# Layer 1's inverse lengths from logarithm and exponential, with three smaller moves between engines

## The chip, the cores and the metric

The kernel runs on one NeuronCore of one Trainium2 chip. The metric is the device time of one execution in microseconds (us), the median over several runs. The kernel's text is in Bass with the Tile framework: the program names tiles and operations, and the framework puts in the semaphores. In some stages the framework also chooses the order of the instructions on an engine; in others the program's own order is kept.

Five engines appear below. PE is TensorE (matrix products; PEld are its weight loads), DVE is VectorE, ACT is ScalarE, POOL is GpSimd, and SP issues most of the DMAs. A float32 matrix product of the program appears in the trace as two MATMUL passes with two weight loads.

## The reference

Four residual layers on x of shape (4, 56, 56, 256) in float32, each over a group-normalised input:

```python
x = x + _L0_conv_ref(_gn(x), ...)   # 7x7 neighbourhood attention, 8 heads
x = x + _L1_conv_ref(_gn(x), ...)   # dense graph over an image's tokens
x = x + _L2_conv_ref(_gn(x), ...)   # neighbourhood attention, two dilations
x = x + _L3_conv_ref(_gn(x), ...)   # shifted 7x7 windows, 8 heads
```

Nearly the whole change lies in layer 1, which sees each image as 3136 tokens of 256 channels:

```python
xn = x / jnp.maximum(jnp.linalg.norm(x, axis=-1, keepdims=True), EPS)   # EPS = 1e-12
A = jnp.einsum('bnc,cc,bmc->bnm', xn, W_adj, xn)
A = jnp.exp(5.0 * (A - jnp.max(A, axis=-1, keepdims=True)))
A = A * (1.0 - jnp.eye(n, dtype=A.dtype))
A = A / jnp.maximum(jnp.sum(jnp.abs(A), axis=-1, keepdims=True), EPS)
rowsum = jnp.sum(A, axis=-1, keepdims=True)
xW = jnp.einsum('bnc,dc->bnd', x, W_aff)
Ax = jnp.einsum('bnm,bmc->bnc', A, x)
AxW = jnp.einsum('bnc,dc->bnd', Ax, W_aff)
diff = rowsum * (xW + b_aff) - AxW
mu = jnp.mean(diff, axis=-1, keepdims=True)
var = jnp.mean((diff - mu) ** 2, axis=-1, keepdims=True)
y = (diff - mu) * jax.lax.rsqrt(var + LN_EPS) * ln_gamma + ln_beta
y = jnp.where(y > 0, y, LEAK * y)
```

The first line divides each token by its length; the lines with `mu` and `var` are a LayerNorm of each token. In layer 0 a query's softmax sum runs over the 49 neighbours, with zero keys outside the image.

## The kernel before

The whole program is one launch. `direct_blocks` computes the four layers one after the other over all four images, with the residual stream in DRAM between them. A flag at the end would start a slower fallback on values out of range; it does not run here.

**Layer 0** works on 128 tiles: 32 groups of seven image rows (`r`), four column tiles each (`t`, with 16, 12, 12 and 16 columns, so 112 or 84 queries). For each tile `attend_pairs` issues the logits (L1080), the exponentials (L1088 and L1090), a multiplication with the mask on POOL (L1091) and, one tile later, the products with the values and with ones (L1113); the product with ones gives the softmax sum. The keys of a tile lie in two pieces. `both` (L1102) adds the two exponentials of a tile on POOL, twice per tile, so that the product with ones need run only once; a tile marked `alone` skips it, and TensorE then runs that product over both pieces. Three tiles are `alone`. The framework chooses the order of the instructions here.

**The tail of layer 0** overlaps the start of layer 1. From group `ALONE` (29 of 0 to 31) on, `stream` takes one entry of the list made by `first_tokens` into the `fill` of each tile. `first_tokens` prepares image 0 of layer 1 in six chunks of 512 tokens and a short one, chunk `NC4`, which holds the last 64 tokens twice. `normal` applies the group norm and squares on ACT (L942, L1397) and adds the two halves of 128 channels on DVE (L1398). `lengths` multiplies the squares with a column of ones (L1406), one product per 128 tokens, which gives the squared lengths as a column; DVE takes a maximum with 1e-24 (L1407), POOL raises it to the power -1/2 (L1408) and writes it on the diagonal of a tile `dg` (L1409). `unit_length` multiplies `dg` by ones (L1425), which brings the inverse lengths to all partitions as a row, and DVE multiplies the tokens by it (L1426). `values` is the product with W_aff (L1418).

**Layer 1** runs over units: a unit is one tile `j` of 128 tokens against up to four tiles from `first` to `last`, and since the matrix is symmetric only `first >= j` is computed. For each unit, TensorE makes logits (L1561), transposes the exponentials (L1669), and multiplies them by `xw` both ways: `by_row` (L1683) into the row's own sum, `by_column` (L1688) into `ps_v`, which DVE adds to `acc` (L1593). ACT takes the exponential (L1564) and copies the transposes (L1672). The main loop, for unit k, does: a small step, the transposes of k, the logits of k+1, a small step, the products of k. After a tile's last unit `finish` makes the LayerNorm: DVE sums, scales and takes the moments (L1726 to L1737), POOL makes the inverse deviation (L1739); two ticks later `normal` subtracts and scales on DVE (L1742), POOL applies gamma and beta (L1743, L1744), and `leaky` (L1747) and `add` (L1754, L1762) follow. A tick comes after each column product.

The chunks of the next image are prepared in between. At `j` of 1, 4, 8, 12, 16, 19 and 23 `replace` loads a chunk, puts its two `normal` steps behind four empty ones in the list `ticks`, and puts its other steps into `small`, due 12 column or row pairs later (`done + 12`): two empty ones, `lengths`, then `values`. `normal` here is DVE (L945), a Square on ACT (L1499) and an addition of halves on POOL (L1500). `lengths` is as in `first_tokens` (L1506 to L1508) for all chunks, but only chunks 3, 4 and 5 take the diagonal and a product with ones (L1516, L1536, due two later). Chunks 0, 1, 2 and `NC4` (`by_dma`) write the inverse lengths to DRAM and read them back on all partitions (L1512, L1513, due 16 later). DVE then multiplies (L1538). If a unit needs a chunk that is not ready, `begin` runs its remaining steps at once. The orders of PE and DVE are the program's in this layer; those of ACT and POOL are chosen by the framework.

PSUM in layer 1 holds one bank `m` (`ps_m`) for small products, two each of `s`, `o` and `v`, and one `t`.

Of the kernel before, what the change touches and what calls it, by code (L numbers as in the profile page):

```python
# [31 lines left out]
NIMG = 4  # L32
# [19 lines left out]
TINY = 1e-12  # L52
NEG = -1e30
# [777 lines left out]
def direct_blocks(ctx: ExitStack, tc: tile.TileContext, d: dict, watch):  # L831
# [8 lines left out]


# [20 lines left out]
    gn_eps = const.tile([P, 1], FP, name="gn_eps")  # L862
    nc.vector.memset(gn_eps, GN_EPS)
    group = const.tile([P, P], FP, name="group")
# [13 lines left out]
    def ps_m():  # L878
        return psum_tile("m", m_bufs)
# [278 lines left out]
    def layer0(early, big, pool, begin_layer1):  # L1158
# [85 lines left out]
        def pair(r, t):  # L1244
# [37 lines left out]
            def quad(hq):  # L1282
                def keys(j, u):
# [6 lines left out]
                 for a in range(2)]  # L1290
            return dict(quads=[quad(0), quad(1)], nk=nk, nq=nq, mask=m[0], emask=m[1], first=gather, done=finish,
                        alone=r == ALONE - 1 and t == 3 or r == ALONE and t == 2 or r == NIMG * NB0 - 1 and t == 3,
# [77 lines left out]

    def first_tokens(few, keep, brief):
# [19 lines left out]
        def normal(c):  # L1391
            m, n, x = part(c)
            sq = box["sq"] = brief.tile([P, CC, 512], FP, tag="sq", name="sq1")
            with tc.issue_after(newest[1].ins):
                for h in range(CC):
                    normalise_act(x[:, h], x[:, h], known(1, 0), h)
            nc.scalar.activation(sq[:, :, :n], x, AF.Square)  # L1397
            nc.vector.tensor_tensor(sq[:, 0, :n], sq[:, 0, :n], sq[:, 1, :n], ALU.add)  # L1398

        def lengths(c):  # L1400
            m, n, x = part(c)
            pm = ps_m()
            rn = few.tile([P, 4, 1], FP, tag="rn", name="rn")
            dg = box["dg"] = few.tile([P, 4, P], FP, tag="dg", name="dg", bufs=1)
            for i in range(m):
                nc.tensor.matmul(pm[:, i:i + 1], lhsT=box["sq"][:, 0, i * P:(i + 1) * P], rhs=ones[:, 0:1], start=True, stop=True)  # L1406
# [15 lines left out]
        def unit_length(c):  # L1422
            m, n, x = part(c)
            pm = ps_m()
            nc.tensor.matmul(pm[:, :n], lhsT=ones, rhs=box["dg"].rearrange("p m k -> p (m k)")[:, :n], start=True, stop=True)  # L1425
            nc.vector.tensor_tensor(x, x, pm[:, :n].rearrange("p (o k) -> p o k", o=1).to_broadcast([P, CC, n]), ALU.mult)  # L1426
# [25 lines left out]
    def layer1(early, big, pool, first, late, next_layer):  # L1452
# [7 lines left out]
        shares = dram.tile([NIMG, (NB + 1) * P], FP, name="shares")  # L1460
# [17 lines left out]
        def tokens(b, c, ps_a=ps_m):  # L1478
# [4 lines left out]
            by_dma = c in (0, 1, 2, NC4)  # L1483
# [18 lines left out]
            def lengths():  # L1502
                pm, sq = ps_a(), box["x0"]
                rn = few.tile([P, 4, 1], FP, tag="rn", name="rn")
                for i in range(m):
                    nc.tensor.matmul(pm[:, i:i + 1], lhsT=sq[:, 0, i * P:(i + 1) * P], rhs=ones[:, 0:1], start=True, stop=True)  # L1506
                nc.vector.tensor_scalar_max(rn[:, :m, 0], pm[:, :m], TINY * TINY)
                nc.gpsimd.tensor_tensor(rn[:, :m, 0], rn[:, :m, 0], mhalf[:, 0:1].to_broadcast([P, m]), ALU.pow)  # L1508
                box["share"] = few.tile([P, 4, P], FP, tag="dg", name="dg", bufs=1)
                if by_dma:  # L1510
                    row = shares[b:b + 1, 4 * c * P:4 * c * P + n]
                    nc.sync.dma_start(out=row.rearrange("o (m p) -> p (o m)", p=P), in_=rn[:, :m, 0])  # L1512
                    nc.sync.dma_start(out=box["share"].rearrange("p m k -> p (m k)")[:, :n], in_=row.to_broadcast([P, n]))  # L1513
                    small.append((done + 16, unit_length, (b, c)))
                else:
                    nc.gpsimd.tensor_tensor(  # L1516
                        box["share"][:, :m, :], ident.rearrange("p (o q) -> p o q", o=1).to_broadcast([P, m, P]),
                        rn[:, :m, :].to_broadcast([P, m, P]), ALU.mult)
                    small.append((done + 2, unit_length, (b, c)))
# [11 lines left out]
            def unit_length():  # L1531

                share = box["share"].rearrange("p m k -> p (m k)")[:, :n]
                if not by_dma:
                    pm = ps_a()
                    nc.tensor.matmul(pm[:, :n], lhsT=ones, rhs=share, start=True, stop=True)  # L1536
                    share = pm[:, :n]
                nc.vector.tensor_tensor(xnT[:, :, 4 * c * P:4 * c * P + n], box["x"][:, :, :n],  # L1538
                                        share.rearrange("p (o k) -> p o k", o=1).to_broadcast([P, CC, n]), ALU.mult)
# [5 lines left out]
            return [load], [lambda h=h: normal(h) for h in range(CC)], [no_step] * 2 + [lengths] + steps  # L1545
# [168 lines left out]
        def finish(b, j):  # L1714
# [19 lines left out]
            mv = late.tile([P, 3], FP, tag="mv", name="mv1", bufs=7)  # L1734
# [85 lines left out]
        def replace(b, c):  # L1820
            if b < NIMG:
# [4 lines left out]
                ticks.extend([no_step] * 4 + normals[b, c])  # L1826
# [693 lines left out]
```

## Time and profile before

| quantity | value |
| --- | --- |
| time, median of 3 runs | 3722.86 us (3720.98 to 3726.05) |
| the profiled execution's own time | 3720.84 us |
| its span, first to last instruction | 3719.0 us |
| mean granted TensorE clock | 0.996 |
| ACT table loads in the trace | 1, of 1283 ns |
| layer 0 up to where `first_tokens` starts | 0 to about 615 us |
| layer 0's tail with `first_tokens` | about 615 to 708 us |
| layer 1 | about 708 to 2560 us |
| layers 2 and 3 | about 2560 to 3719 us |

In a group row of the profile, the numbers after the shapes are the count, the busy time in us and the mean duration of one in ns, then the idle time of the engine just before them and what ended it. In rows in order of time the first two columns are start and length in us; a bracket at the end gives the idle time before and its releaser. A busy TensorE overlaps its own passes, so what an instruction really occupies is read from start to next start.

### The profile page before, as it was taken

Reading aid. Unit: us, or ns where it says so; the run is one execution under the profiler, and the core shown is the slowest. Engines: PE = TensorE matmul, PEld = TensorE weight load, DVE = VectorE, ACT = ScalarE, POOL = GpSimd, SP = SyncE. Lnnn points to the kernel's source line nnn. Section 1 sums busy time; section 2 is a strip of 40 time slices with the busy share of each in tenths; the row PEclk is TensorE's granted clock in tenths of the full one; section 3 lists DMA queues with packets and bytes.
Section 4 is the critical chain, followed back from the end, with each engine's and each line's share of the span. In section 5 each row is a group of like instructions: output and inputs, shape, how many; then the busy total and the mean of one; then the engine's idle time right before and its main releaser. Section 6 shows DMA issues by size and latency. Waiting matters only on the chain.

```text
span 3719.0 us, 112489 instructions
## 1 busy us (share of the span) xinstructions
PE 3645.2 (98%) x48938; PEld 2480.5 (67%) x48938; DVE 2197.2 (59%) x4176; ACT 1479.4 (40%) x3137; POOL 1802.9 (48%) x1952
## 2 busy tenths in 40 slices
PE   8999999999999999999999999999999999999998
PEld 4666666677776777767777777776666666555554
DVE  5787777544445444554444643445777777677776
ACT  5666665422222222222222222223666666444443
POOL 4777777421235222352222521124877778455555
PEclk9999999999999999999999999999999999999999
DMA  6554444300011000100000000002455444544443
GB/s 223 167 162 138 142 127 139 112 7 24 23 29 33 18 19 19 30 28 23 19 19 23 28 15 11 11 20 78 121 139 145 135 135 127 157 135 133 132 133 100
DMA packets 278695, 304.95 MB, mean 82 GB/s; under 512 B 33670, under 2 KB 269578, under 8 KB 277838
## 3 DMA queue, kind: packets, MB, share of 16 engines
q1 hardware_dynamic: 276336, 297.43, 26.6%
q8 instruction: 386, 6.32, 0.7%
q0 software_dynamic: 1568, 0.16, 0.1%
q14 instruction: 117, 0.96, 0.1%
q10 hardware_dynamic: 288, 0.08, 0.0%
HBM read 205.04 MB, written 92.55 MB: 80 GB/s over the span
## 4 chain that ended last, share of the span: by engine, by line
PE 90%; DVE 4%; POOL 1%; DMA 1%; issue 1%; ACT 1%; SPq 0%; DVEq 0%; ACTq 0%; POOLq 0%
PE ps_m L952 19%; PE ps_o L1683 14%; PE ps_s L1561 14%; PE ps_v L1688 13%; PE ps_m L981 7%; PE ps_o L1113 6%; PE ps_s L1080 6%; PE ps_t L1669 3%; PE ps_o L1040 2%; PE ps_s L1024 1%; PE ps_m L1526 1%; DMA vp<-vd 1%; POOL b L1102 1%; PE ps_m L1418 1%; PE ps_m L1754 1%
## 5 line engine op out<-in xcount | busy, mean ns | idle before, releaser
L1593 DVE TENSOR_TENSOR acc<-acc,ps_v 128x257 f32<-128x257 f32 x1088 | 457.5, 422 | 774.8 <-PE ps_v L1688 751.8
L1688 PE MATMUL ps_v<-xw,e 128*128 128x257 f32 x2208 | 611.1, 381 | 3.5 <-DVE xnT L1538 2.2
L1683 PE MATMUL ps_o<-xw,at 128*128 128x257 f32 x2208 | 609.0, 379 | 0.0
L1561 PE MATMUL ps_s<-xnT,xd 128*128 128x512 f32 (+3 forms) x1344 | 571.4, 548 | 3.9 <-DVE xnT L1538 3.9
L1672 ACT COPY at<-ps_t 128x512 f32<-128x512 f32 (+3 forms) x332 | 170.4, 513 | 953.6 <-PE ps_t L1669 953.4
L1688 PEld LDWEIGHTS ps_v<-xw,e 128*128 128x128 f32 x2208 | 413.4, 189 | 145.0 <-issue 83.2
L1102 POOL TENSOR_TENSOR b<-e 124x448 f32<-124x448 f32 (+5 forms) x498 | 484.7, 994 | 7.2 <-PE ps_o L1113 0.3
L1683 PEld LDWEIGHTS ps_o<-xw,at 128*128 128x128 f32 x2208 | 419.1, 190 | 60.1
L952 PE MATMUL ps_m<-xn,w_wqkv 128*32 128x392 f32 x4096 | 374.3, 494 | 2.3 <-PE ps_s L1080 1.1
L1554 POOL TENSOR_SCALAR xd<-xnT,vec 128x128 f32<-128x128 f32 x192 | 116.1, 614 | 475.6 <-PE ps_s L1561 475.4
L1564 ACT ACTIVATE e<-ps_s 128x512 f32<-128x512 f32 x336 | 185.3, 552 | 354.4 <-PE ps_s L1561 351.1
L1561 PEld LDWEIGHTS ps_s<-xnT,xd 128*128 128x128 f32 x1344 | 225.4, 191 | 141.4 <-issue 126.2
L1091 POOL TENSOR_TENSOR e<-e,m0t 126x672 f32<-126x672 f32 (+3 forms) x128 | 238.7, 1865 | 158.6 <-ACT e L1090 126.2
L1091 POOL TENSOR_TENSOR e<-e,bias 119x784 f32<-119x784 f32 (+5 forms) x128 | 241.7, 1888 | 151.6 <-ACT e L1090 150.8
L1113 PEld LDWEIGHTS ps_o<-e,vp 124*32 124x32 f32 (+3 forms) x8192 | 198.0, 110 | 104.4 <-issue 85.3
L1002 ACT ACTIVATE no<-rs 128x168 f32<-128x168 f32 (+2 forms) x256 | 93.9, 367 | 385.8 <-DVE rs L2008 185.9
L952 PEld LDWEIGHTS ps_m<-xn,w_wqkv 128*32 128x32 f32 x4096 | 124.3, 109 | 176.5 <-issue 128.7
L2008 DVE RECIPROCAL rs<-ps_o 128x196 f32<-128x196 f32 (+2 forms) x128 | 175.7, 1373 | 103.6 <-PE ps_o L1113 83.4
L1113 PE MATMUL ps_o<-e,vp 124*32 124x112 f32 (+3 forms) x8192 | 227.6, 248 | 4.2 <-DMA vp<-vd 3.9
L1088 ACT ACTIVATE e<-e 126x672 f32<-126x672 f32 (+5 forms) x256 | 219.6, 858 | 17.4 <-DVE e L1087 5.0
L1090 ACT ACTIVATE e<-ps_s 126x672 f32<-126x672 f32 (+5 forms) x256 | 206.1, 805 | 8.6 <-PE ps_s L1080 6.4
L981 PE MATMUL ps_m<-w_wqkv,xn 128*32 128x256 f32 x3136 | 197.6, 381 | 3.8 <-DVE xr L2044 2.0
(235 smaller groups left out, 5973.6 us busy)
## 6 DMA issues: line engine op xcount, KB each, us to landing
x<-xr SPq DMA_DIRECT2D x64, 392.0 KB
x<-in_x SPq DMA_DIRECT2D x53, 448.0 KB
x<-x SPq DMA_DIRECT2D x60, 392.0 KB
xr<-x SPq DMA_DIRECT2D x60, 392.0 KB
vd<-v SPq DMA_DIRECT2D x72, 256.0 KB
xr<-in_x SPq DMA_DIRECT2D x32, 392.0 KB
xr<-x SPq DMA_DIRECT2D x28, 448.0 KB
x<-xr SPq DMA_DIRECT2D x28, 448.0 KB
```

What stands on the lines that cost most here:

```text
L952: nc.tensor.matmul(pm[j * HD:(j + 1) * HD, :n], lhsT=w[:, h, col + j * HD:col + (j + 1) * HD], rhs=rhs(h), start=(h == 0), stop=(h == CC - 1))
L981: nc.tensor.matmul(pm[i:i + HD, j * C:(j + 1) * C], lhsT=xn[:, h, first + i:first + i + HD], rhs=w[:, h, :], start=(h == 0), stop=(h == CC ...
L1080: nc.tensor.matmul(s[j // 2][:nk, j % 2, (2 * i + u) * nq:(2 * i + u + 1) * nq], lhsT=k(j, u), rhs=q(j), start=True, stop=True)
L1088: newest.append(nc.scalar.activation(ev, ev, AF.Exp))
L1090: nc.scalar.activation(ev, sv, AF.Exp)
L1091: nc.gpsimd.tensor_tensor(parts(ev), parts(ev), w["emask"], ALU.mult)
L1102: nc.gpsimd.tensor_tensor(w["b"][a][:nk, :, :2 * nq].rearrange("p h (i c) -> p h i c", i=2), ev[:, :, :, 0, :], ev[:, :, :, 1, :], ALU.add)
L1113: nc.tensor.matmul(w["o"](k, i)[j * HD:(j + 1) * HD], lhsT=ones[:nk, :HD] if k else v(j, u), rhs=w["b"][j // 2][:nk, j % 2, i * nq:(i + 1) ...
L1561: nc.tensor.matmul(s[:, :n], lhsT=xd[j][:, h, :], rhs=xnT[:, h, first * P:last * P], start=(h == 0), stop=(h == CC - 1))
L1593: nc.vector.tensor_tensor(acc[:, i, :], acc[:, i, :], pv[:, :C + 1], ALU.add)
L1683: nc.tensor.matmul(out[j][:, :C + 1], lhsT=e[:, col(i)] if i == j else at[:, col(i)], rhs=xw[:, i, :], start=(i == j), stop=(i == NB - 1))
L1688: nc.tensor.matmul(pv[:, :C + 1], lhsT=e[:, col(i)], rhs=xw[:, j, :], start=True, stop=True)
```

## The change

It has four parts and one load.

- **Lengths.** In both token paths the squares are multiplied by a full 128x128 tile of ones, so that the squared lengths come out on all partitions as a row at once. `inverse_lengths` takes Ln, with the argument scaled by 2^16, and then Exp of -1/2 times that plus 8 ln 2, on ACT. `shorten` takes the minimum with 1e12 and multiplies the tokens, in one DVE instruction. The maximum, the power, the diagonal, the second product and the way over DRAM go.
- **Halves.** In `first_tokens` the addition of the two halves on DVE goes; TensorE accumulates both halves in its product. In layer 1's `tokens` the addition on POOL stays.
- **Layer 0's last sums.** `alone` holds for the last 13 tiles, from group 28's last tile on, instead of for three.
- **LayerNorm.** `normal` in `finish` becomes one ACT instruction with a scale and a bias per token; POOL makes the bias, minus mean times inverse deviation.
- **Due times.** `unit_length` is due four pairs after `lengths` for all chunks, with an empty step behind `lengths`. The last chunk's `normal` comes after two empty ticks instead of four, and its other steps are due 7 pairs later instead of 12, without the two empty ones ahead of `lengths` (these also go for the short chunk).
- **Table load.** An explicit load of the ACT table set `natural_log_exp_and_others` is the first instruction of ACT.

```diff
+    tables = [s.name for s in act_sets.SETS].index("natural_log_exp_and_others")
+    nc.scalar.add_instruction(mybir.InstLoadActFuncSet(name=nc.get_next_instruction_name(), act_func_set_id=tables,
+                                                       ins=[], outs=[]))
...
-    gn_eps = const.tile([P, 1], FP, name="gn_eps")
+    offsets = const.tile([P, 2], FP, name="offsets")
+    gn_eps, half_ln = offsets[:, 0:1], offsets[:, 1:2]
     nc.vector.memset(gn_eps, GN_EPS)
+    nc.vector.memset(half_ln, LN_SCALE / 2 * float(np.log(2.0)))
...
-                        alone=r == ALONE - 1 and t == 3 or r == ALONE and t == 2 or r == NIMG * NB0 - 1 and t == 3,
+                        alone=NTC * r + t >= NTC * ALONE - 1,
...
+    def inverse_lengths(share, pm):
+        nc.scalar.activation(share, pm, AF.Ln, scale=float(2 ** LN_SCALE))
+        nc.scalar.activation(share, share, AF.Exp, scale=-0.5, bias=half_ln)
+
+    def shorten(dst, x, share):
+        n = share.shape[1]
+        nc.vector.scalar_tensor_tensor(dst, share.rearrange("p (o k) -> p o k", o=1).to_broadcast([P, CC, n]), 1 / TINY, x,
+                                       ALU.min, ALU.mult)
...
@@ first_tokens @@
             nc.scalar.activation(sq[:, :, :n], x, AF.Square)
-            nc.vector.tensor_tensor(sq[:, 0, :n], sq[:, 0, :n], sq[:, 1, :n], ALU.add)
...
-            for i in range(m):
-                nc.tensor.matmul(pm[:, i:i + 1], lhsT=box["sq"][:, 0, i * P:(i + 1) * P], rhs=ones[:, 0:1], start=True, stop=True)
-            nc.vector.tensor_scalar_max(rn[:, :m, 0], pm[:, :m], TINY * TINY)
-            nc.gpsimd.tensor_tensor(rn[:, :m, 0], rn[:, :m, 0], mhalf[:, 0:1].to_broadcast([P, m]), ALU.pow)
-            nc.gpsimd.tensor_tensor(dg[:, :m, :], ident.rearrange("p (o q) -> p o q", o=1).to_broadcast([P, m, P]),
-                                    rn[:, :m, :].to_broadcast([P, m, P]), ALU.mult)
+            for h in range(CC):
+                nc.tensor.matmul(pm[:, :n], lhsT=ones, rhs=box["sq"][:, h, :n], start=(h == 0), stop=(h == CC - 1))
+            box["share"] = few.tile([P, 4 * P], FP, tag="share", name="share", bufs=1)
+            inverse_lengths(box["share"][:, :n], pm[:, :n])
...
@@ tokens @@
+                nc.tensor.matmul(pm[:, :n], lhsT=ones, rhs=sq[:, 0, :n], start=True, stop=True)
+                box["share"] = few.tile([P, 4 * P], FP, tag="share", name="share", bufs=1)
+                inverse_lengths(box["share"][:, :n], pm[:, :n])
+                small.append((done + 4, unit_length, (b, c)))
...
+                shorten(xnT[:, :, 4 * c * P:4 * c * P + n], box["x"][:, :, :n], box["share"][:, :n])
...
-            return [load], [lambda h=h: normal(h) for h in range(CC)], [no_step] * 2 + [lengths] + steps
+            return [load], [lambda h=h: normal(h) for h in range(CC)], [no_step] * (2 if c < NC4 - 1 else 0) + [lengths, no_step] + steps
...
@@ finish @@
+            nc.gpsimd.tensor_scalar(mv[:n, 3:4], mv[:n, 0:1], rstd[:n], -1.0, ALU.mult, ALU.mult)
...
-                nc.vector.tensor_scalar(y, y, mv[:n, 0:1], rstd[:n], ALU.subtract, ALU.mult)
+                nc.scalar.activation(y, y, AF.Identity, bias=mv[:n, 3:4], scale=rstd[:n])
...
@@ replace @@
-                ticks.extend([no_step] * 4 + normals[b, c])
-                small[:0] = [(done + 12, step, (b, c)) for step in steps]
+                soon = c == NC4 - 1
+                ticks.extend([no_step] * (2 if soon else 4) + normals[b, c])
+                small[:0] = [(done + (7 if soon else 12), step, (b, c)) for step in steps]
```

More of the change, by code (lines that the diff above doesn't have):

```diff
@@ L20 @@
 import concourse.tile as tile
-from concourse import mybir
+from concourse import act_sets, mybir
 from concourse._compat import with_exitstack
@@ L52 @@
 TINY = 1e-12
+LN_SCALE = 16
 NEG = -1e30
@@ L1402, in lengths @@
             pm = ps_m()
-            rn = few.tile([P, 4, 1], FP, tag="rn", name="rn")
-            dg = box["dg"] = few.tile([P, 4, P], FP, tag="dg", name="dg", bufs=1)
-            for i in range(m):
-                nc.tensor.matmul(pm[:, i:i + 1], lhsT=box["sq"][:, 0, i * P:(i + 1) * P], rhs=ones[:, 0:1], start=True, stop=True)
-            nc.vector.tensor_scalar_max(rn[:, :m, 0], pm[:, :m], TINY * TINY)
-            nc.gpsimd.tensor_tensor(rn[:, :m, 0], rn[:, :m, 0], mhalf[:, 0:1].to_broadcast([P, m]), ALU.pow)
-            nc.gpsimd.tensor_tensor(dg[:, :m, :], ident.rearrange("p (o q) -> p o q", o=1).to_broadcast([P, m, P]),
-                                    rn[:, :m, :].to_broadcast([P, m, P]), ALU.mult)
+            for h in range(CC):
+                nc.tensor.matmul(pm[:, :n], lhsT=ones, rhs=box["sq"][:, h, :n], start=(h == 0), stop=(h == CC - 1))
+            box["share"] = few.tile([P, 4 * P], FP, tag="share", name="share", bufs=1)
+            inverse_lengths(box["share"][:, :n], pm[:, :n])
         def values(c, i0):
@@ L1423, in unit_length @@
             m, n, x = part(c)
-            pm = ps_m()
-            nc.tensor.matmul(pm[:, :n], lhsT=ones, rhs=box["dg"].rearrange("p m k -> p (m k)")[:, :n], start=True, stop=True)
-            nc.vector.tensor_tensor(x, x, pm[:, :n].rearrange("p (o k) -> p o k", o=1).to_broadcast([P, CC, n]), ALU.mult)
+            shorten(x, x, box["share"][:, :n])
             if c == NC4:
@@ L1459, in layer1 @@
         racc = big.tile([P, C + 1], FP, name="racc")
-        shares = dram.tile([NIMG, (NB + 1) * P], FP, name="shares")
         idx = big.tile([98, WN], I32, name="idx")
@@ L1482, in tokens @@
             n = m * P
-            by_dma = c in (0, 1, 2, NC4)
             box = {}
@@ L1503, in lengths @@
                 pm, sq = ps_a(), box["x0"]
[L1504 to L1519, printed above, removed]
+                nc.tensor.matmul(pm[:, :n], lhsT=ones, rhs=sq[:, 0, :n], start=True, stop=True)
+                box["share"] = few.tile([P, 4 * P], FP, tag="share", name="share", bufs=1)
+                inverse_lengths(box["share"][:, :n], pm[:, :n])
+                small.append((done + 4, unit_length, (b, c)))
             def values(i0):
@@ L1531, in unit_length @@
             def unit_length():
[L1533 to L1539, printed above, removed]
+                shorten(xnT[:, :, 4 * c * P:4 * c * P + n], box["x"][:, :, :n], box["share"][:, :n])
                 if c == NC4:
@@ L1733, in finish @@
             st = pool.tile([P, 6], FP, tag="st", name="st1")
-            mv = late.tile([P, 3], FP, tag="mv", name="mv1", bufs=7)
+            mv = late.tile([P, 4], FP, tag="mv", name="mv1", bufs=7)
             nc.vector.bn_stats(out=st[:n], in_=y)
```

## The prediction

> **What bounds the kernel now.** I read the page's first part, then the busy time by stage, then TensorE's waits inside the two stages that the change touches, then the instructions in order of time. First the page, its engines and its chain:
>
> ```profile
> PE 3645.2 (98%) x48938; PEld 2480.5 (67%) x48938; DVE 2197.2 (59%) x4176; ACT 1479.4 (40%) x3137; POOL 1802.9 (48%) x1952
> PE 90%; DVE 4%; POOL 1%; DMA 1%; issue 1%; ACT 1%; SPq 0%; DVEq 0%; ACTq 0%; POOLq 0%
> ```
>
> TensorE is busy for all but 74 us and makes 90% of the chain. Two things can move the time: TensorE work added or removed, and those 74 us with what they do to its clock. By stage (core 0: length, then busy time and instructions of PE, PEld, DVE, ACT, POOL, then granted clock, DMA share, GB/s):
>
> ```profile
> 0.00:615.00 615.00, 590.40 (x13476) 366.92 (x13480) 453.72 (x671) 378.93 (x891) 450.83 (x380) 1.00 0.50 156
> 615.00:708.00 93.00, 85.66 (x1410) 61.59 (x1402) 62.95 (x94) 46.00 (x83) 61.88 (x53) 0.93 0.33 102
> 708.00:2560.00 1852.00, 1837.98 (x8270) 1361.51 (x8271) 859.80 (x2225) 419.63 (x790) 537.94 (x796) 1.00 0.09 24
> ```
>
> The second row is layer 0's tail, where `first_tokens` runs; the third is layer 1. The tail has 7.3 us of idle TensorE (93.00 less 85.66) and a clock of 0.93, worth another 6.5 us (93 x 0.07). Layer 1 has 14.0 us idle, 12.4 of it in three like stretches, one at each image's end (4.23 in 1100 to 1230, 4.23 in 1570 to 1700, 3.95 in 2045 to 2170), with ACT busy 23% of the stage. TensorE's waits in the tail (total, times, longest) and two 5 us slices of the tail:
>
> ```profile
> PE ps_m L1406 <- DVE sq L1398: 3.5, 4, 1.2
> PE ps_m L1418 <- DVE xnT L1426: 1.3, 2, 1.0
> ...
> 635.00:640.00 5.00, 3.78 (x74) 3.26 (x78) 3.21 (x6) 2.80 (x4) 5.00 (x5) 0.91 0.52 154
> 640.00:645.00 5.00, 5.00 (x33) 4.08 (x30) 2.36 (x3) 2.72 (x6) 5.00 (x6) 0.50 0.29 99
> ```
>
> The largest wait is for the very addition of halves that the change takes from DVE. After the gaps before 640 the clock falls to 0.50, with POOL full.
>
> **The change, part by part.** Times are of the profiled execution: span 3719.0, its own time 3720.84, 2.0 below the median 3722.86.
>
> *Lengths in layer 1.* One matrix product of the program is two passes in the trace. The first image boundary shows both prices:
>
> ```profile
> 1146.54 1.02 PE L1536 MATMUL ps_v<-dg,ones 128*128 128x512 f32 x2
> 1147.39 0.49 PE L1669 MATMUL ps_t<-ident,e 128*128 128x128 f32 x3
> ...
> 1213.30 0.95 PE L1506 MATMUL ps_m<-ones,x 128*128 128x1 f32 x8
> 1214.11 0.64 PE L1669 MATMUL ps_t<-ident,e 128*128 128x128 f32 x4
> ...
> 1220.37 1.98 PE L1561 MATMUL ps_s<-xnT,xd 128*128 128x512 f32 x4 [1.31 <-DVE xnT L1538]
> ```
>
> From start to next start, four one-column products take 0.81 us, one 512-wide product 0.85. For images 1 to 3, chunks 3 to 5 go from 0.81 + 0.85 to 0.85: nine times -0.81, -7.3. Chunks 0, 1, 2, which had no wide product, go from 0.81 to 0.85: nine times +0.04, +0.4. In image 0 six chunks go from 1.66 to two wide products, 1.70: +0.2. The short chunks come out even. TensorE in layer 1: **-6.7**.
>
> *What hangs on it.* DVE's maximum (L1507, 0.16), POOL's power and diagonal (L1508, L1516, 1.02 and 1.04) and 24 DMA issues (L1512, L1513, 0.36 and 0.33 each on SP) go. They cost nothing today: the DMA share is 0.09 and the result was due 16 products later. ACT gains Ln and Exp, by the 128x512 Exp of L1564 (0.60 each): 1.2 us a chunk, 28 chunks, 34 us. Ln waits for the wide product. Behind it on ACT stand the copy of the transposes (L1672) and Exp of the logits (L1564), for which TensorE's row products and the next transposes wait. The cover: after its transposes TensorE has 1.72 us of logits and one column product (0.43) before it needs the copy. Where the next unit is one tile wide its logits take 0.45, and about 0.5 us is exposed; I charge +1.0 in all (0 to 34). `unit_length` on DVE now waits for ACT instead of TensorE; behind it stand the additions L1593, which free `ps_v` for L1688. Four products of distance (a row and a column product together 0.87 us) cover the 1.2 us. Its multiply (L1538, 1.21) becomes a three-operand one from SBUF; three-operand L1732 at 486 ns against two-operand L1742 at 426 for 256 elements suggests up to 14% more, 0.17 us x 21, hidden but at the boundaries.
>
> *Boundary stalls.* The last chunk's normalisation comes two ticks and its other steps five products sooner. Today they are forced one after the other between 1213 and 1220, ending in the 1.31 us wait above; with the work due earlier I take that off three times, -3.9 (0 to -3.9). The x tile is there: its load waits only for a buffer. Of the remaining 8.5 us, which wait for DVE (L1762, L1538, L1593), I take 2.6 off, a third, because DVE loses 0.43 us per tile (next part). Together **-6.5**, ends -12.4 and 0.
>
> *LayerNorm on ACT.* 100 multiplies leave DVE (L1742, 426 ns, 42 us) and enter ACT. ACT's L942 takes 703 ns at 392 and 753 at 448 elements with the same two vector operands, so 0.58 at 256: 58 us; ACT goes from 23% to 28% with the lengths. POOL gets 100 small products, 0.23 each by L926. All lies under TensorE's 98%. Only at the end of layer 1, where the trace's chain runs through POOL's L1739, L1743 and L1744 (2566 to 2573), is there less cover: 0.23 more on POOL and 0.15 on ACT, **+0.3**.
>
> *Layer 0's tail.* 13 tiles instead of 3 skip `both`. Ten tiles save 20 POOL additions (L1102, 0.9 to 1.15 us, 20 us of the 62 there), and TensorE sums both halves itself:
>
> ```profile
> 649.18 0.57 PE L1113 MATMUL ps_o<-b,ones 124*32 124x112 f32 x16
> 649.68 1.12 PE L1080 MATMUL ps_s<-q,kI 32*126 32x84 f32 x32
> ...
> 693.73 0.95 PE L1113 MATMUL ps_o<-e,ones 95*32 95x112 f32 x32
> 694.61 3.72 PE L1418 MATMUL ps_m<-w_waff,xnT 128*128 128x256 f32 x16
> ```
>
> 0.88 against 0.50 at 112 columns, +0.38; the same reading at 84 columns is 0.69 against 0.40, +0.29. Five tiles of each: **+3.4**.
>
> *The tail's stalls.* DVE's addition of halves ended 0.4, 1.1, 1.25 and 0.8 us after the Square that feeds it; without it the 3.5 us of waits fall by 2.7. POOL's 20 us of relief should take another 1.0 of the 7.3 us. I take **-3.7** (ends -7.3, 0). What is late next is the arrival of data: the chain there has 6.8 us of `vp` and 5.8 us of `xnT` transfers, which stay. If half the gaps go, I take half of the clock's loss with them, **-3.2**; ends -6.5 and +3.4 (one more half-clock stretch like that before 646).
> The Trainium skill, "TensorE: Matmul & The Clock Gate", section "HAM oscillation — how this bites in real kernels", puts the re-throttling at TensorE gaps above about 3.4 us. The longest wait here is 1.2 us and the clock fell all the same, so I keep the row; by the rule closing such gaps would return no clock, and the sum below would be -11.7.
>
> *The start.* The table load (1283 ns, now after ACT's two DMA issues) is put ahead of them, so `vec` lands 1.28 later, 5.4 instead of 4.1, and DVE's first statistics wait behind `qbias` until 5.55 instead of 4.89, less 0.24 of idle after it: **+0.5** (0 to 1.3).
>
> Sum: -6.7 + 1.0 - 6.5 + 0.3 + 3.4 - 3.7 - 3.2 + 0.5 = -14.9. 3720.8 becomes 3705.9; by the median 3722.9 it is **3708 us**.
>
> **The rivals.** *Only the arithmetic counts (3720).* Stalls move and do not shrink, since layer 0 is ordered by the framework anew and DVE still has its 4 us chains at the boundaries: -6.7 + 3.4 + 0.5 = -2.8. For it: waits of 0.2 to 1.3 us with seven different releasers. Against it: the largest is removed work.
> *ACT becomes late (3733 to 3747).* If the Ln/Exp pair stands uncovered in front of L1672, each of 28 chunks costs 1.2 us. With no boundary gain the rest is -6.7 + 0.3 + 3.4 - 3.7 - 3.2 + 0.5 = -9.4: slower than before from 8 uncovered chunks, beyond the measurement from 14 (+7.4); all 28 give +24, 3747; sixteen give +10, 3733. For it: strict order on ACT, one `m` bank, short units at the image ends. Against it: ACT idles 330 us before L1564 and 564 us before L1672.
> *The one table does not hold (up to 3780).* If Ln and Exp each load a table, 56 loads of 1283 ns are 72 us of ACT in the same place: 3708 + 72 = 3780 if exposed, 3708 if hidden. The trace has one load in all and cannot show it.
> The skill's "ScalarE: Activation LUTs", section "Table sets: the hidden batching unit", says that one set holds both functions and needs one load; no run here shows that yet.
>
> **How the numbers follow.** 0.2% is 7.4 us, about what a measurement of this kernel can tell from no change: faster is below 3715.4, slower above 3730.3. Forecast 0.64, arithmetic alone 0.18, ACT late 0.15, tables 0.03. Faster 0.64, same 0.19, slower 0.17. With every end at its best (-6.7 - 12.4 + 0.3 + 3.4 - 7.3 - 6.5 = -29.2) it is 3694; the forecast's own range is 3697 to 3715. Reaching over the arithmetic to the foot of the ACT case gives 3695 to 3730.
>
> **What would show it.** Right: no L1742 on DVE; one table load; about 150 one-column passes less in layer 1; layer 1's idle TensorE under 9 us, the 1.3 us wait for `xnT` gone; the tail's idle near 4 us at a clock near 0.96. Wrong: TensorE waiting for L1672's or L1564's successors behind Ln; further table loads; a tail with a lower clock; a layer 0 that is longer before 615.

## The result and the profile after

The changed kernel takes 3725.35 us (median of 19 runs, 3720.54 to 3731.55) against 3717.98 us for the kernel before (19 runs, 3714.01 to 3726.05): a ratio of 1.0018, 95% interval 1.0012 to 1.0024. It is slower, by about 7 us, where 3708 us and a gain were forecast. The profiled execution took 3724.74 us with a span of 3722.9.

The page's engines and its chain, after:

```profile
PE 3635.9 (98%) x48936; PEld 2464.1 (66%) x48936; DVE 2154.7 (58%) x4042; ACT 1562.6 (42%) x3293; POOL 1771.6 (48%) x1988
PE 90%; DVE 4%; ACT 1%; POOL 1%; DMA 1%; issue 1%; SPq 0%; DVEq 0%; ACTq 0%; POOLq 0%
```

TensorE works 9.3 us less than before, and the span is 3.9 us longer: what was saved came back as idle time. The two stages, in the same columns as in the prediction:

```profile
615.00:708.00 93.00, 84.58 (x1546) 59.42 (x1538) 62.92 (x84) 55.31 (x103) 29.84 (x23) 1.00 0.38 120
708.00:2560.00 1852.00, 1825.42 (x8104) 1344.83 (x8103) 817.15 (x2096) 489.39 (x920) 534.67 (x855) 1.00 0.07 22
```

In the tail the granted clock is 1.00 where it was 0.93, and POOL has 29.84 us of work where it had 61.88. In layer 1 TensorE idles 26.6 us (1852.00 less 1825.42) where it idled 14.0. Fixed slices shift against the work when something ahead gets shorter, so the stages are also told by the same instructions in both traces. Layer 1 runs from its first short unit's logits to its last row product:

| kernel | layer 1 begins | layer 1 lasts | layers 2 and 3 | span |
| --- | --- | --- | --- | --- |
| before | 708.7 | 1855.4 | 1154.9 | 3719.0 |
| after | 701.4 | 1865.4 | 1156.1 | 3722.9 |

The tail gained 7.3 us, layer 1 lost 10.0, and the layers after it 1.2. TensorE's waits in layer 1 (total, times, longest) tell where:

```profile
PE ps_m L1745 <- DVE xr L1753: 7.1, 6, 1.9
PE ps_m L1512 <- POOL x L1508: 6.0, 2, 3.0
PE ps_v L1678 <- DVE acc L1583: 3.8, 3, 1.5
PE ps_s L1551 <- DVE xnT L1385: 3.6, 3, 1.2
PE ps_v L1512 <- POOL x L1508: 3.0, 1, 3.0
```

New is the wait of the product of ones (L1512, the old L1506) for POOL's addition of halves: 3.0 us at each of the three image ends. The transposes of y wait 7.1 us for DVE's additions into `xr` where they waited 3.8 (L1745 and L1753 are the old L1754 and L1762). The wait for `xnT`, forecast to go, went from 3.9 to 3.6. The first image end in order of time shows the new one:

```profile
1192.70 1.00 DVE L951 TENSOR_SCALAR xn<-x,gst 128x512 f32<-128x512 f32 x2
1193.73 1.06 ACT L1507 ACTIVATE x<-xn 128x1024 f32<-128x1024 f32 x1 [3.37 <-DVE xn L951]
1194.87 1.26 POOL L1508 TENSOR_TENSOR x<-x 128x512 f32<-128x512 f32 x1 [7.54 <-ACT x L1507]
1196.18 1.13 PE L1512 MATMUL ps_m<-x,ones 128*128 128x512 f32 x2 [2.98 <-POOL x L1508]
```

The normalisation, the Square and the addition take 3.4 us one after the other (1192.70 to 1196.13). ACT and POOL were idle before theirs, and each starts within 0.1 us of what feeds it: the chain itself is the wait. TensorE stands from 1193.20. A slice just behind it, in the window view's columns:

```profile
1197.50:1200.90 3.40, 3.40 (x7) 1.50 (x6) 0.00 (x0) 1.65 (x3) 0.00 (x0) 0.50 0.59 154
```

For 3.4 us the granted clock is 0.50, which costs another 1.7 us. Layer 1 of the kernel before has no such slice; this one has two at the first image end. Between the first and the last instruction of layer 1 TensorE idles 13.5 us before and 27.5 after, which is 14.0 more, and is busy 1841.96 and 1837.88, which is 4.1 less with the half-clock time in it: together the 10.0 us. The waits account for the idle time: 9.0 (POOL) + 3.3 (`xr`) + 2.6 (`acc`) + 1.2 (copies into `acc`, not among the rows above) - 2.5 (`xnT`, for which the column products also waited 2.2 before) = 13.6.

### The profile page after: what moved, and what is told of

Same layout as the page of the kernel before. It is cut to its first block, busy times and chain, and to the rows that moved or that the text cites. A ratio compares the mean times of both kernels' runs of the same rounds, so it can differ in the third digit from the quotient of the medians.

```text
span 3722.9 us, 112433 instructions
## 1 busy us (share of the span) xinstructions
PE 3635.9 (98%) x48936; PEld 2464.1 (66%) x48936; DVE 2154.7 (58%) x4042; ACT 1562.6 (42%) x3293; POOL 1771.6 (48%) x1988
## 4 chain that ended last, share of the span: by engine, by line
PE 90%; DVE 4%; ACT 1%; POOL 1%; DMA 1%; issue 1%; SPq 0%; DVEq 0%; ACTq 0%; POOLq 0%
PE ps_m L958 19%; PE ps_s L1551 14%; PE ps_o L1673 14%; PE ps_v L1678 13%; PE ps_m L987 7%; PE ps_o L1119 6%; PE ps_s L1086 6%; PE ps_t L1659 3%; PE ps_o L1046 2%; PE ps_s L1030 1%; PE ps_m L1522 1%; PE ps_o L1637 1%; PE ps_s L1593 1%; PE ps_m L1745 1%; DMA vp<-vd 1%
## 5 line engine op out<-in xcount | busy, mean ns | idle before, releaser
L1108 POOL TENSOR_TENSOR b<-e 124x448 f32<-124x448 f32 (+4 forms) x478 | 463.9, 992 | 6.6
```

What stands on the lines that cost most here:

```text
L1108: nc.gpsimd.tensor_tensor(w["b"][a][:nk, :, :2 * nq].rearrange("p h (i c) -> p h i c", i=2), ev[:, :, :, 0, :], ev[:, :, :, 1, :], ALU.add)
```

## The experiments

Ratios are to the kernel before, timed on the same chip in the same batch, with 95% intervals. Medians of two kernels that are set beside each other can be of two batches; the kernel before had medians of 3716.9 to 3718.3 us in them. "Kernel 6" is the kernel of experiment 6. Line numbers move by a few between kernels.

**1. The old timing of the last chunk**, all else as changed.

```diff
-                soon = c == NC4 - 1
-                ticks.extend([no_step] * (2 if soon else 4) + normals[b, c])
-                small[:0] = [(done + (7 if soon else 12), step, (b, c)) for step in steps]
+                ticks.extend([no_step] * 4 + normals[b, c])
+                small[:0] = [(done + 12, step, (b, c)) for step in steps]
...
-            return [load], [lambda h=h: normal(h) for h in range(CC)], [no_step] * (2 if c < NC4 - 1 else 0) + [lengths, no_step] + steps
+            return [load], [lambda h=h: normal(h) for h in range(CC)], [no_step] * 2 + [lengths, no_step] + steps
```

> The changed kernel with the last chunk's old timing alone: its normal steps after four empty ticks, its other steps due 12 pairs later, two empty steps ahead of lengths (for the short chunk too). Theory A (the last chunk's lengths were pulled ahead of POOL's addition of halves, 3.0 us of idle TensorE at each of three boundaries, and the clock fell after it): the wait of the lengths product for POOL goes, about 9 us and some clock come back, 3713 to 3716, at or below the kernel before (3718). Rival B (the Ln/Exp pair or LayerNorm on ACT, or the bank held by Ln, costs the time): 3722 or more, since all of these stay. Rival C (the tail of layer 0 or the table load is dearer than the profiled execution shows): 3722 or more too.

Measured: 3714.49 us (11 runs), ratio 0.9990 (0.9981 to 0.9999), 10.9 us under the change's 3725.35 of another batch. The wait for POOL is gone: DVE's L951 now runs at 1196.15 and 1197.03, POOL's addition ends at 1200.0, and TensorE asks for it only at 1203.86. Being done earlier was of no use, since TensorE asked earlier still. But layer 1 lasts 1857.0 us, 1.6 more than before, so 6.7 us of removed products still bring nothing.

**2. The empty steps alone.** The change as it is, with only the two empty steps ahead of `lengths` back.

```diff
-            return [load], [lambda h=h: normal(h) for h in range(CC)], [no_step] * (2 if c < NC4 - 1 else 0) + [lengths, no_step] + steps
+            return [load], [lambda h=h: normal(h) for h in range(CC)], [no_step] * 2 + [lengths, no_step] + steps
```

> The changed kernel with only the two empty steps ahead of lengths put back; the last chunk stays due 7 pairs later and its normal steps after two empty ticks. Theory A: lengths moves one unit (about 6 us) behind POOL's addition, the 3.0 us waits go, and the chunk is still done before its first logits: 3709 to 3714, faster than the kernel before and than the variant with all of the old timing. Rival B: 3722 or more.

Measured: 3717.22 us (11 runs), ratio 1.0002 (0.9993 to 1.0011). The wait for POOL goes here too, so it was the missing empty steps that made TensorE ask too soon; the gain of 8.1 us is less than was expected. The waits for `xr` (7.1) and `xnT` (5.7) are those of experiment 1.

**3. The tail alone.** The kernel before, with the 13 tiles, the new `lengths` of `first_tokens` and the table load; layer 1 as before.

```diff
+                        alone=NTC * r + t >= NTC * ALONE - 1,
...
@@ first_tokens @@
-            nc.vector.tensor_tensor(sq[:, 0, :n], sq[:, 0, :n], sq[:, 1, :n], ALU.add)
...
+            for h in range(CC):
+                nc.tensor.matmul(pm[:, :n], lhsT=ones, rhs=box["sq"][:, h, :n], start=(h == 0), stop=(h == CC - 1))
...
+            inverse_lengths(box["share"][:, :n], pm[:, :n])
...
+            shorten(x, x, box["share"][:, :n])
```

> The kernel before with the changes to layer 0's tail and the table load alone: 13 alone tiles and the new lengths of first_tokens; layer 1's later chunks and LayerNorm as before. Theory A: layer 1 begins about 7 us earlier than in the kernel before's profiled execution, as in the changed kernel's (701 against 709), and 4 to 7 us of it are left at the end: ratio 0.998 to 0.999. Rival C: no gain or a loss, ratio 1.000 or above.

Measured: 3711.55 us (11 runs), ratio 0.9983 (0.9974 to 0.9992). Layer 1 begins 8.7 us earlier and then keeps before's length within 0.4 us (1855.1). This half of the change is a gain, and layer 1 hands it on whole; the medians of the batch show 6.7 us of it.

**4. The 13 tiles alone.** The kernel before with that one line.

```diff
-                        alone=r == ALONE - 1 and t == 3 or r == ALONE and t == 2 or r == NIMG * NB0 - 1 and t == 3,
+                        alone=NTC * r + t >= NTC * ALONE - 1,
```

> The kernel before with one edit: 13 tiles instead of 3 at the end of layer 0 leave out POOL's additions and let TensorE sum both halves. Theory A (POOL's relief carries the tail): of the 8.65 us that the tail gained with both edits, 6 or more appear here although TensorE has 3.4 us more work, POOL is no longer full in 635 to 645 and the clock stays at 1.0; median about 3712. Theory B (the halves' addition and the diagonal in the lengths carry it): the tail gains 2 us or loses up to 3, and the clock still falls there; median 3716 to 3721.

Measured: 3720.64 us (11 runs), ratio 1.0008 (0.9999 to 1.0017): no gain, and layer 1 begins 2.0 us later. The first of two slices of its tail holds the clock's fall, the second is all in it:

```profile
625.00:635.00 10.00, 8.24 (x227) 6.61 (x224) 7.96 (x12) 6.79 (x15) 4.01 (x3) 0.87 0.84 283
635.00:640.00 5.00, 5.00 (x42) 4.11 (x44) 2.18 (x4) 3.14 (x6) 3.58 (x5) 0.50 0.52 154
```

POOL has room now (3.58 of 5.00, where it was full), and the clock falls all the same. So the full POOL was not what made the tail slow; the new `lengths` carry the gain. Experiment 11 asks the same from the other side.

**5. LayerNorm on ScalarE alone**, in the kernel before.

```diff
+            nc.gpsimd.tensor_scalar(mv[:n, 3:4], mv[:n, 0:1], rstd[:n], -1.0, ALU.mult, ALU.mult)
...
-                nc.vector.tensor_scalar(y, y, mv[:n, 0:1], rstd[:n], ALU.subtract, ALU.mult)
+                nc.scalar.activation(y, y, AF.Identity, bias=mv[:n, 3:4], scale=rstd[:n])
```

> The kernel before with LayerNorm's scaling on ACT alone. Theory A: hidden, within 2 us of the kernel before (ratio 0.9995 to 1.0005), perhaps 1 us less of TensorE's waits for DVE at the boundaries. Rival B: the new order on ACT and POOL costs 3 us or more, ratio above 1.0008.

Measured: 3737.87 us (5 runs), ratio 1.0053 (1.0039 to 1.0066): 19.6 us slower than before in the same batch. The largest wait of TensorE in layer 1, and the first image end:

```profile
PE ps_v L1633 <- ACT xw L961: 8.6, 3, 3.6
```

```profile
1177.56 0.58 POOL L1739 TENSOR_TENSOR mv<-mv,mhalf 128x1 f32<-128x1 f32 x1
1178.11 1.02 POOL L1508 TENSOR_TENSOR rn<-rn,mhalf 128x4 f32<-128x4 f32 x1
1179.09 0.44 POOL L1566 TENSOR_TENSOR e<-e,offd 128x128 f32<-128x128 f32 x1
1179.53 0.26 POOL L1740 TENSOR_SCALAR mv<-mv 128x1 f32<-128x1 f32 x1
...
1179.82 0.60 ACT L1743 ACTIVATE y<-y,mv 128x256 f32<-128x256 f32 x1 [4.42 <-POOL mv L1740]
1180.33 0.56 ACT L961 COPY xw<-ps_v 128x512 f32<-128x512 f32 x1
...
1180.94 0.48 PE L1633 MATMUL ps_v<-xw,e 64*128 64x257 f32 x1 [3.61 <-ACT xw L961]
```

Read from the bottom: TensorE waits 3.61 us for `ps_v`, which ACT's copy (L961) empties. ACT was idle for 4.42 us, and the products that the copy takes had ended at 1176.7, yet the copy did not run: in front of it stood the LayerNorm's scaling (L1743), which waited for POOL's bias (L1740), and between POOL's power (L1739) and the bias stood the power for the lengths (L1508) and another product, 1.5 us. An idle engine's queue was blocked at its head. In the changed kernel L1508's power is gone and this wait with it.

**6 and 7. LayerNorm back on DVE** in the changed kernel (7), and in it with the old timing (6). The edit is the reverse of that of experiment 5.

> The changed kernel with the last chunk's old timing, and LayerNorm's subtract and multiply back on DVE as in the kernel before; the tail of layer 0 and layer 1's Ln/Exp lengths stay as changed. Theory A (LayerNorm on ScalarE is what keeps layer 1 from its 6.7 us: it stands in ACT's order in front of work that TensorE waits for, as it did when it was tried alone): layer 1 becomes about 6 us shorter than before's 1855.4, the waits of the transposes of y for xr fall from 7.1 to about 4, median 3703 to 3707. Theory B (the shortening multiply now stands on DVE in front of the LayerNorm's additions, and TensorE's product that used to cover them is gone; LayerNorm on ACT is a help): the waits for xr stay at 7 us or grow, layer 1 stays near 1855 to 1858, median 3710 to 3718.

> The changed kernel with only LayerNorm's subtract and multiply back on DVE; the last chunk keeps its earlier timing. Theory A (the earlier timing is a cost by itself): the 3.0 us waits for POOL's addition of halves stay at all three image ends, as long as before, and the time stays some 8 to 10 us over that of the kernel with the old timing and LayerNorm on DVE. Theory B (POOL's queue was late because of the LayerNorm's additional small product on POOL): the wait falls below 1.5 us and the two kernels agree within 3 us.

Measured: with the old timing 3711.71 us (11 runs), ratio 0.9983 (0.9974 to 0.9992); with the early timing 3721.50 (11 runs), ratio 1.0007 (0.9998 to 1.0016). The three waits of 3.0 us for POOL stay in the second and not in the first, 9.8 us apart: the timing costs by itself, whoever does the LayerNorm. Inside layer 1 the LayerNorm's place makes no difference now (1856.8 against 1857.0 in experiment 1), and the waits for `xr` stay at 7.1. What holds them? The trace of the first of the two, first image end:

```profile
1176.93 1.22 DVE L1385 SCALAR_TENSOR_TENSOR xnT<-share,xn 128x1024 f32<-128x1024 f32 x1
1178.07 0.41 DVE L1752 TENSOR_TENSOR xr<-xr,ps_m 128x256 f32<-128x256 f32 x1
...
1178.54 0.44 PE L1744 MATMUL ps_m<-ident,y 128*128 128x128 f32 x2 [1.86 <-DVE xr L1752]
```

```profile
1205.90 0.72 ACT L1380 ACTIVATE share<-share,offsets 128x512 f32<-128x512 f32 x1
...
1208.82 0.69 DVE L965 COPY xw<-ps_m 128x512 f32<-128x512 f32 x1 [5.13 <-PE ps_m L1522]
1209.43 1.21 DVE L1385 SCALAR_TENSOR_TENSOR xnT<-share,xn 128x1024 f32<-128x1024 f32 x1
...
1210.69 0.70 PE L1551 MATMUL ps_s<-xnT,xd 128*128 128x512 f32 x1 [1.91 <-DVE xnT L1385]
```

In the first, the multiply by the lengths stands on DVE just in front of the addition into `xr` that the next transposes wait for. In the second, the factors are ready at 1206.6 and DVE is idle, but the multiply stands behind the copy of the values (L965), which waits for TensorE until 1208.8. Before, the multiply had to stand there, because its factors came through the second product; that product also gave TensorE 0.85 us of work shortly ahead of the first of these waits and during the second (in the trace before, L1536 at 1184.67 and at 1218.03).

**8 and 9. The multiply moved.** Kernel 6 with the multiply of the last chunk put in front of its values (8), and with those of the last two whole chunks (9).

```diff
-                small.append((done + 4, unit_length, (b, c)))
+                small.insert(0 if NC4 - 2 <= c < NC4 else len(small), (done + 4, unit_length, (b, c)))
```

(In 8 the condition is `c == NC4 - 1`.)

> The kernel with layer 0's tail and layer 1's Ln/Exp lengths as changed, the last chunk's old timing and LayerNorm on DVE, with one edit: for the last chunk the shortening multiply stands on DVE in front of the copy of the values and no longer behind it. Its factors are ready some 2.3 us after the product of ones, while TensorE still has 3.4 us of values. Theory A (the saved product used to cover DVE's order, and the order alone eats the gain): the three waits of the logits for xnT (5.7 us in all, 1.9 each) fall below 0.5 us each, the half-clock stretches after them (at 1211 and 1686) go, layer 1 is 5 to 9 us shorter, median 3703 to 3708. Theory B (DVE has a fixed chain at the image's end that TensorE meets wherever the multiply stands): the 1.9 us reappear as waits for the additions into acc or for xr, and the median stays at 3710 to 3713.

> The same edit for the last two whole chunks: the multiply of the last but one also moves, from just in front of the LayerNorm's addition into xr to an earlier place, and one of its two value products moves on TensorE to a place just in front of the transposes of y. Theory A: besides the waits for xnT, the waits of the transposes of y for xr fall from 7.1 us to 4 or less; median 3699 to 3705, some 3 us below the kernel with the last chunk alone moved. Theory B: the waits for xr stay at 6 to 7 us, since the LayerNorm's chain on DVE is as long as before, and the time is that of the kernel with the last chunk alone moved, within 2 us.

Measured: 3703.21 us (5 runs), ratio 0.9965 (0.9952 to 0.9979), and 3695.52 us (5 runs), ratio 0.9943 (0.9929 to 0.9957). The same instructions in another order: 16 us below kernel 6 in the medians, which are of another batch, and 15.2 in the length of layer 1. Kernel 9 is faster than either of its expectations had it. In 8 the waits for `xnT` are gone from layer 1; in 9 the waits of the transposes for `xr` fall too, from 7.1 us, with 1.3 of them now for a copy. In 9 one value product of TensorE has also come to stand just ahead of these transposes, and how much of the fall is due to it and how much to DVE's order was not separated.

```profile
PE ps_v L1678 <- DVE acc L1583: 5.0, 6, 1.5
PE ps_m L1744 <- DVE xr L1752: 1.5, 3, 0.5
...
PE ps_m L1744 <- DVE xw L965: 1.3, 1, 1.3
```

The same place as above in kernel 9, where the multiply runs while TensorE makes the values, and the logits follow without a wait:

```profile
1204.93 1.23 DVE L1385 SCALAR_TENSOR_TENSOR xnT<-share,xn 128x1024 f32<-128x1024 f32 x1 [2.97 <-ACT share L1380]
...
1207.09 0.69 DVE L965 COPY xw<-ps_m 128x512 f32<-128x512 f32 x1 [0.94 <-PE ps_m L1522]
```

**10. Order and timing, order and LayerNorm.** The move of experiment 9 put into the changed kernel (10a), and into the kernel of experiment 1 (10b, old timing, LayerNorm on ScalarE).

> The changed kernel itself (early last chunk, LayerNorm on ScalarE) with only the order of the shortening multiplies of the last two whole chunks changed, as in the kernel before this one. Theory A (two faults, independent of each other: the early timing waits for POOL, the order waits for DVE): the waits for xnT and for xr fall as they did, the three waits of 3.0 us for POOL's addition of halves stay, median 3703 to 3712. Theory B (the order is the whole fault, and the POOL wait was only its consequence): the POOL wait falls below 1 us too, median 3694 to 3700.

> The best kernel so far (tail, Ln/Exp lengths, old timing, multiplies moved) with LayerNorm's scaling on ScalarE as in the change. Theory A (with POOL's power and diagonal of the lengths gone, ACT's turn is not late and LayerNorm there is free): within 3 us of 3695.5, no wait of TensorE for ACT's copy of the values. Theory B (LayerNorm on ACT costs wherever it stands, as it did alone with +19.6 us): 3 us or more above, with waits for ACT's copies at the image ends.

Measured: 10a 3714.72 us (11 runs), ratio 0.9991 (0.9982 to 1.0000); 10b 3701.21 us (5 runs), ratio 0.9955 (0.9941 to 0.9968). In 10a the three waits of 3.0 us for POOL stand as they were, and those for `xnT` and `xr` fall: order and timing are two faults, independent of each other, as theory A has it, though the time lies 2.7 us above A's range. 10b is 5.7 us over kernel 9 in the medians of two batches, as theory B has it, but not through the image ends, as B says: layer 1 agrees within 0.3 us (1841.9 against 1841.6). The loss lies just behind its last row product, in the column of layers 2 and 3 of the table below. In 10b, with ACT's turn there:

```profile
2541.82 0.26 POOL L1730 TENSOR_SCALAR mv<-mv 128x1 f32<-128x1 f32 x1
2542.12 0.60 ACT L1733 ACTIVATE y<-y,mv 128x256 f32<-128x256 f32 x1 [2.52 <-POOL mv L1730]
2542.63 1.91 ACT L948 ACTIVATE xn<-x,gst 128x392 f32<-128x392 f32 x3
...
2543.38 0.88 PE L958 MATMUL ps_m<-xn,w_wqkv 128*32 128x392 f32 x4 [2.00 <-ACT xn L948]
```

Layer 2's first normalisation (L948) stands behind the LayerNorm's scaling of one of the last tiles, which waits 2.52 us for POOL; TensorE waits 2.00 us, and in kernel 9 0.86. Half-clock time follows at 2543.4. It is the mechanism of experiment 5 at the one place where it is left. The longer wait (1.1 us) and the half-clock time (3.4 us, worth 1.7) make 2.8 us at this place. Three pairs that differ only in LayerNorm's engine have medians 2.8 (experiments 1 and 6), 3.9 (after and 7) and 5.7 us apart (10b and 9), all in this direction, but each pair is of two batches and the intervals of its ratios overlap; what is above 2.8 is not shown.

**11. Three tiles again.** Kernel 9 with the old condition for `alone`.

> The best kernel so far (tail with Ln/Exp lengths, old timing, LayerNorm on DVE, multiplies of the last two whole chunks moved) with one edit back: 3 tiles at the end of layer 0 leave out POOL's additions instead of 13, so TensorE has 3.4 us less work there and POOL 20 us more. Theory A (the 13 tiles cost TensorE time and only the lengths relieve the tail): layer 1 begins 2 to 4 us earlier, median 3692 to 3694. Theory B (with the lengths changed, POOL's relief counts): layer 1 begins 2 us or more later, with TensorE waiting for POOL's additions and a half-clock stretch in 630 to 690; median 3697 to 3702.

Measured: 3693.92 us (5 runs), ratio 0.9936 (0.9923 to 0.9950), 24.0 us below the kernel before in the same batch; layer 1 begins 3.7 us earlier than in kernel 9, about what the 13 tiles' extra products were costed at (3.4). The tail's slice:

```profile
615.00:708.00 93.00, 84.56 (x1377) 58.09 (x1375) 65.10 (x87) 55.77 (x106) 51.97 (x42) 1.00 0.41 135
```

POOL is busy 51.97 us again, and the clock is 1.00. In the medians the two kernels are 1.6 us apart with overlapping intervals, so only the start of layer 1 tells them apart. This is the fastest version found: the new lengths in both paths (with the table load, the halves summed on TensorE in `first_tokens`, and `unit_length` due after four pairs), everything else as before, and the multiplies moved.

The same instructions compared across all kernels:

| kernel | layer 1 begins | layer 1 lasts | layers 2 and 3 | waits for POOL in layer 1 |
| --- | --- | --- | --- | --- |
| 1, old timing | 700.5 | 1857.0 | 1156.6 | none |
| 2, empty steps | 703.0 | 1860.3 | 1154.3 | none |
| 3, tail alone | 700.0 | 1855.1 | 1151.9 | none |
| 4, 13 tiles alone | 710.7 | 1855.2 | 1152.7 | none |
| 5, LayerNorm alone | 708.8 | 1873.4 | 1152.2 | none |
| 6, 1 without LayerNorm | 700.5 | 1856.8 | 1154.0 | none |
| 7, after without LayerNorm | 701.6 | 1868.2 | 1150.8 | 9.0 us |
| 8, 6 with one multiply moved | 699.6 | 1850.2 | 1150.8 | none |
| 9, 6 with two moved | 700.8 | 1841.6 | 1151.3 | none |
| 10a, after with two moved | 700.1 | 1855.8 | 1154.2 | 9.0 us |
| 10b, 1 with two moved | 699.5 | 1841.9 | 1156.6 | none |
| 11, 9 with three tiles | 697.2 | 1841.7 | 1151.3 | none |

## Why the prediction was wrong

The forecast's sum was -14.9 us in the profiled span; it became +3.9. The step that failed is **"Boundary stalls: -6.5"**. It took the early timing of the last chunk for a relief of the 1.31 us wait; the runs show it to be the largest single cost of the change, 9.8 to 13.5 us (three pairs of medians: after and 1, 7 and 6, 10a and 10b). The step argued that the x tile is there and stopped; it never laid the chain of DVE, ACT and POOL (3.4 us in the rows of the profile after) against the moment at which TensorE would now ask. The same step gave DVE's relief 2.6 us (called a third of 8.5, which would be 2.8); the LayerNorm on ScalarE gave none inside layer 1 (experiments 1 and 6 agree within 0.2 us), since it is DVE's order there, not its load, that TensorE waits for.

*Lengths in layer 1, -6.7.* The products did go: TensorE's busy time from the first to the last instruction of layer 1 is 1841.96 us before and 1831.74 in kernel 9, 10.2 less. Counted from each start to the next start, the products of the lengths themselves go from 23.2 us to 16.1, which is 7.1 less and near the term; the other 3.1 us lie with the instructions beside them, and the runs do not say why. In the changed kernel half-clock time hides part of it. But removing a product removes cover, too: with the early timing gone, layer 1 was 1.4 us longer than before (kernel 6) until the multiply was moved. With it moved layer 1 is 13.8 us shorter, which is near the forecast's -6.7 and -6.5 together, by a route that the forecast did not name.

*Ln and Exp, +1.0.* Ln takes 597 ns and Exp 724, together 1.3 us where 1.2 were costed. In layer 1 of the changed kernel one wait of TensorE is for an Exp of the logits, 0.7 us at its start, and it was there before too; none is for the copy of the transposes. No cost is to be seen there, and the rival in which the pair stands uncovered on ACT falls; in the tail there is one such wait (below). That rival's mechanism was real, one instruction further on: the LayerNorm's scaling blocked ACT's queue.

*LayerNorm at the end of layer 1, +0.3.* Mis-sized. It was costed by the lengths of its instructions; the price is that of what stands behind them on ACT, 2.8 us at that place in kernel 10b.

*The tail, +3.4 - 3.7 - 3.2 = -3.5.* Right in sign, too small: -7.3 in the changed kernel, -8.7 alone. From the same TensorE instruction of layer 0 to the beginning of layer 1, before and after:

```profile
611.50:708.70 97.20, 89.20 (x1490) 63.94 (x1479) 66.34 (x98) 48.40 (x89) 65.19 (x57) 0.93 0.34 104
...
610.20:701.40 91.20, 83.48 (x1615) 59.59 (x1604) 63.66 (x82) 55.81 (x103) 31.20 (x22) 1.00 0.36 111
```

TensorE idles 8.0 us before and 7.7 after, so the -3.7 for its waits did not come. Those for DVE's halves (3.5) went, but in the changed kernel TensorE waits 1.7 us for the Square in their place, 1.9 for Ln (L1379), which holds `ps_m`, and 2.3 where the profile names no releaser. What came back is the clock: 13.7 us of half-clock time before, worth 6.8, and none after, where half of the loss was forecast. That is not certain either, for experiments 2 and 7, with the same tail, have one stretch of 3.4 us near 635. The 13 tiles' products cost what was said (+3.7 by experiment 11), but POOL's relief gave nothing for them.

*The start, +0.5.* None. The table load stands ahead of ACT's transfers and did not hold them up:

```profile
0.73 1.28 ACT L843 ACT_TABLE_LOAD   x1 [0.73 <-PEq L2485]
...
0.76 0.42 ACTq L854 DMA_DIRECT2D vec<-in_vec  x1
```

ACT's queue issued the transfer of `vec` 0.03 us after the load began. TensorE starts at 13.5 us here and at 13.8 to 14.1 in experiments 1, 3, 6 and 9, all with the load, against 14.0 before.

*The table.* One load in the whole trace, with Ln and Exp in turn 28 times: the rival with a load for each falls. The Trainium skill's "ScalarE: Activation LUTs", section "Table sets: the hidden batching unit", says that one set has both functions and needs one load; the trace agrees.

*The chances.* Of the forecast and its rivals, *only the arithmetic counts* (3720) came nearest in time, but by luck: the removed products did give back their time, and new stalls were made, which it does not have.

## What to carry to other kernels

Work that is taken from the engine that sets the pace was also the cover of a handover on the others. Before counting the saving, write down for each removed product who was working under it, and move what waited for its result to where the result now comes earlier. An instruction put on an idle engine costs what stands behind it in that engine's queue while it waits for its operands. And a step that is asked for sooner needs its whole chain sooner, not only its first load.

## What the runs showed of the hardware

**The clock.** In layer 1 half-clock time came in stretches of 3.4 us or twice that, and at its image ends each of them began between 1.1 us before the end of a wait and 1.6 us after it. There no wait up to 1.5 us was followed by one (before and experiments 3, 4, 9, 10b and 11 have no longer ones there), of 36 waits of 1.9 to 3.0 us (after and experiments 1, 2, 6, 7, 8 and 10a) 15 were, and both waits of 3.6 us in experiment 5 were. The Trainium skill's "TensorE: Matmul & The Clock Gate", section "HAM oscillation — how this bites in real kernels", puts the re-throttling at gaps above some 3.4 us; here 1.9 us sufficed, and 3.0 us did not always.

The traces show what tells these waits apart. In each of the fourteen traces all changes of the granted clock lie on a grid of 3.413 us. With layer 1 cut into the cells of that grid, all 17 falls of the clock came after a cell in which TensorE was busy for 0.16 to 0.45 of the time, and of the other cells, over 7000, only three were as low (0.42, 0.43 and 0.45). A wait of 1.5 us leaves at least 0.56 of a cell; one of 1.9 us can leave as little as 0.44 where it falls into one cell; one of 3.0 us can be split between two. In the changed kernel, the cell ahead of the fall at 1197.47 (1.29 of 3.41 us busy), and the two cells that share the wait from 2145.15 to 2148.13, which no fall followed:

```profile
1194.06:1197.47 3.41, 1.29 (x5) 0.76 (x6) 0.00 (x0) 0.86 (x2) 1.26 (x1) 1.00 0.00 0
2142.97:2146.38 3.41, 2.18 (x11) 1.55 (x9) 2.47 (x7) 0.69 (x1) 0.00 (x0) 1.00 0.00 0
2146.38:2149.79 3.41, 1.66 (x7) 1.07 (x8) 0.00 (x0) 0.86 (x2) 1.26 (x1) 1.00 0.00 0
```

A slice of kernel 6 behind its wait of 1.91 us:

```profile
1211.50:1214.90 3.40, 3.40 (x7) 1.79 (x6) 0.29 (x1) 0.60 (x1) 1.09 (x2) 0.50 0.00 0
```

In the tail of layer 0 the busy share does not tell them apart: the clock fell after cells with up to 0.73 (before, at 639.1) and did not after some with 0.44 (experiment 6, at 679.0). What decides there is open.

**Layers that were not touched.** Layers 2 and 3 last between 1150.8 and 1156.6 us in these traces. Of the kernels with new lengths in layer 1, the five with LayerNorm on ScalarE have a mean of 1155.6 and the five with it on DVE 1151.6. The rest of the spread goes in part with half-clock stretches near 3140 to 3210 us (none in kernel 11, 10.2 us of them in the kernel before), and no edit reaches there. A gain of a few microseconds should be read from the stage that was changed before it is read from the end.
